# One of eight products of a selective scan moved from VectorE to GpSimd, its operand spread by transfers

## The chip, the core and the metric

The kernel runs on one core of a Trainium2 chip. The metric is device time in microseconds (us) of one execution. Engines are called as in the profile: PE (TensorE), DVE (VectorE), ACT (ScalarE), POOL (GpSimd), SP (SyncE, which here only issues transfers).

## What is computed

A chain of four layers on x of shape (2, 128, 64, 64), fp32: a Mamba-like sequence layer with two blocks, two convolutional attention layers, and a multi-scale fusion. The change lies in the first, of which this is what matters (B = 2 images, L = 4096 tokens, di = 256 inner channels, N = 16 states):

```python
dt, Bm, Cm = jnp.split(u @ xproj_w.T, [R, R + N], axis=-1)
dt = jax.nn.softplus(dt @ dt_w.T + dt_b)
dA = jnp.exp(dt[..., None] * A)
dBu = (dt * u)[..., None] * Bm[:, :, None, :]
def step(h, inp):
    dA_t, dBu_t, C_t = inp
    h = dA_t * h + dBu_t
    y = jnp.einsum('bdn,bn->bd', h, C_t)
    return (h, y)
...
y = ys.transpose(1, 0, 2) + u * ssm_D
y = y * jax.nn.silu(z)
```

Before it stand a layer norm, a projection to u and z and a causal convolution of four taps; after it a projection, a residual, a second layer norm and a feed-forward part with GELU.

## The kernel before

The sequence layer is cut into 32 chunks of 512 tokens: 2 images x 2 blocks x 8 chunks, in this order (`items`). A chunk has 256 x 16 = 4096 pairs of channel and state. They are dealt with in eight *steps* of 512 pairs: a step takes 32 channels (`k = 32 * (s_ % 4)` of half `s_ // 4`), and its tile `h` of 128 partitions x 4 x 512 tokens holds four groups of 32 partitions, each with all 32 channels, times four `m`: 16 states in all. So an operand that depends on channels alone has to be spread, four copies of 32 partitions under one another. For `dt` transfers do that (`spread_dt`, four per step, lines 373 to 378). For dt * u (`dtu`) PE does it, with a matrix of zeros and ones as stationary operand, into the PSUM tile `pdu`, of which there is one (`spread_dtu`, lines 380 to 383). B and C come spread from DRAM in the tiles `bb` and `cb` (`spread_bc`, lines 345 to 354).

A step has four *slots*, one for each `m`; a chunk has 32. Per step: DVE multiplies `bb` by `pdu` into `h` (`times_b`, line 389). Per slot: ACT makes `da`, the exponential of dt times A, four slots ahead into one of four PSUM buffers (`decay`, line 396), and DVE runs the scan along the 512 tokens in place in `h` (`scan`, line 407). At a step's last slot POOL copies the last column as the carry for the next chunk (line 409) and multiplies `h` by `cb` in place (line 410). PE then sums over states, for two steps at a time, into `py` (`y_pair`, line 422, 16 matmul records a pair).

The order on every engine is written out by hand. `slot(i, todo, t_)` issues, for slot t_ of chunk i: at the first slot of a step `spread_dt` for three steps ahead and `spread_dtu` for one ahead, at every second step `y_pair` of the steps three and two back; then the scan, the `decay` of four slots ahead, at the last slot of a step `times_b` of the next step; and last what `background(i)` has put at that slot. So `times_b` of step s stands in slot 4s - 1, and `y_pair` of steps (0, 1), (2, 3), (4, 5), (6, 7) in slots 12, 20, 28 and slot 4 of the next chunk. The background holds the work of neighbouring chunks, among it:

- slots 0 to 5: the convolution of the next chunk (`pu_taps`, line 310), and z of this one (line 323)
- slot 7: `y_out` (line 430) and `gate` on POOL (line 433) of the chunk before; slots 3 to 12: the rest of the feed-forward part of the chunk two back, whose tile `hid` is read last in slot 7 (`ffn_down`, line 467)
- slot 11: `silu`; slots 12 to 15: layer norms (`pc`, line 244), `xproj` (line 339) and its copy `dbl` (line 343), and from it on SP the transfers `dr`, `bb` (slot 14) and `cb` (slot 22)
- slots 15 to 18: `dtproj` (`pt`, line 358), the softplus on ACT (line 364), `dt_end` on POOL (`dtu`, line 370), all for the next chunk
- slots 17 to 21: the variance (`var`, line 258) and reciprocal root of the layer norms, with two small products on POOL (`nt`, line 274, `rs`, line 279) and one step on ACT between (line 275); slots 27 to 29: their spread on PE (`pr`, line 283), the scaling on DVE (line 287) and the shift on ACT (line 300)
- slots 30 and 31: the first half of the feed-forward part (`ffn_up`, line 455) into a new `hid`

The tiles `h` and `hid` share one tag with five buffers, which are handed out in turn: a new one takes the buffer of the fifth allocation before it, and its first writer waits for that one's last reader. A chunk allocates eight `h` and one `hid`.

Ahead of the first chunk stands a prologue (i = -2 and -1) that also loads the 3x3 weights of the next layer (`load_rest`, into three of the five `h` buffers) and folds them on DVE (`fold`, lines 190 to 206, in slots 8 to 10 of i = -1); the folded weights are written to DRAM.

Of the kernel before, what the change touches and what calls it, by code (L numbers as in the profile page):

```python
# [6 lines left out]
F32 = mybir.dt.float32  # L7
AF = mybir.ActivationFunctionType
ALU = mybir.AluOpType
# [4 lines left out]
B, C, H, W = 2, 128, 64, 64  # L14
N = H * W
P = 128
CH = 512
# [50 lines left out]
def tile_conv_seq(ctx: ExitStack, tc, x, consts, vecs, wemb, wlay, wconv, wdt, wqkv, wsmall, wms, out):  # L68
    nc = tc.nc
# [46 lines left out]
    with tc.manual_schedule(), ExitStack() as s:  # L116
# [4 lines left out]
        sp = scans.enter_context(tc.tile_pool(name="l0s", bufs=1, side="right"))  # L121
        bc = scans.enter_context(tc.tile_pool(name="l0bc", bufs=1, space=PSUM, side="right"))
# [15 lines left out]
        def four(g):  # L138
            return fsel[:, g].rearrange("p q d -> p (q d)")
# [30 lines left out]
                nc.vector.tensor_tensor(u[:, k, :], cw[:, KC, :], cw[:, k, :], ALU.mult)  # L170
            wu.append(u), am.append(a)

        raws = []

        def load_rest():
            for which in range(3):
# [13 lines left out]
        def fold(which):  # L190

            g = [raws[which][:, :, k, :] for k in range(3)]
            lo, hi = (sp.tile([P, 3, 3, C], F32, name=n, tag="h", bufs=5) for n in ("ulo", "uhi"))
            tt, ts, stt = nc.vector.tensor_tensor, nc.vector.tensor_scalar, nc.vector.scalar_tensor_tensor
            tt(lo[:, 1], g[0], g[2], ALU.add)
            ts(lo[:, 1], lo[:, 1], -1.0 / 6, None, ALU.mult)
            stt(lo[:, 0], g[1], 1.0 / 6, lo[:, 1], ALU.mult, ALU.add)
            stt(lo[:, 1], g[1], -1.0 / 6, lo[:, 1], ALU.mult, ALU.add)
            stt(hi[:, 0], g[2], 4.0, g[0], ALU.mult, ALU.add)
            ts(hi[:, 0], hi[:, 0], 1.0 / 24, None, ALU.mult)  # L200
            stt(lo[:, 2], g[1], -1.0 / 12, hi[:, 0], ALU.mult, ALU.add)
            stt(hi[:, 0], g[1], 1.0 / 12, hi[:, 0], ALU.mult, ALU.add)
            ts(hi[:, 1], g[0], 0.25, None, ALU.mult)
            nc.vector.tensor_copy(hi[:, 2], g[2])
            for k, u in enumerate((lo, hi)):
                nc.sync.dma_start(ufold[which][:, 9 * k : 9 * k + 9, :], u.rearrange("p s y c -> p (s y) c"))


# [4 lines left out]
        NI, NST, NSL = len(items), 8, 32  # L213
        st = [{} for _ in items]
# [3 lines left out]
        def has(i):  # L218
            return 0 <= i < NI
# [153 lines left out]
        def spread_dt(g):  # L373
            i, s_ = divmod(g, NST)
            o = st[i]["dtb", s_] = sp.tile([P, CH], F32, name="dtb", tag="dtb", bufs=4)
            k = 32 * (s_ % 4)
            for q in range(4):
                nc.sync.dma_start(o[32 * q : 32 * q + 32, :], st[i]["dt"][k : k + 32, s_ // 4, :])

        def spread_dtu(g):  # L380
            i, s_ = divmod(g, NST)
            pdu = st[i]["pdu", s_] = bc.tile([P, CH], F32, name="pdu", tag="bc")
            nc.tensor.matmul(pdu, lhsT=four(s_ % 4), rhs=st[i]["dtu"][:, s_ // 4, :], start=True, stop=True)  # L383

        def times_b(g):
            i, s_ = divmod(g, NST)
            h = st[i]["h", s_] = sp.tile([P, 4, CH], F32, name="h", tag="h", bufs=5)
            pdu = st[i].pop(("pdu", s_))
            nc.vector.tensor_tensor(h, st[i]["bc", 0], pdu.unsqueeze(1).to_broadcast([P, 4, CH]), ALU.mult)  # L389
# [8 lines left out]
        def scan(t):  # L398
            g, m = divmod(t, 4)
            i, s_ = divmod(g, NST)  # L400
            j, gg = divmod(s_, 4)
            b, l, c = items[i]
            if (b, l) not in carries:
                carries[b, l] = sp.tile([P, NJ, 4, 4], F32, name="carry", tag="carry", bufs=2)
                nc.gpsimd.memset(carries[b, l], 0.0)
            h, da = st[i]["h", s_], st[i].pop(("da", s_, m))
            nc.vector.tensor_tensor_scan(h[:, m, :], da, h[:, m, :], carries[b, l][:, j, gg, m : m + 1], ALU.mult, ALU.add)  # L407
            if m == 3:
                nc.gpsimd.tensor_copy(carries[b, l][:, j, gg, :].unsqueeze(2), h[:, :, CH - 1 : CH])  # L409
                nc.gpsimd.tensor_tensor(h, h, st[i]["bc", 1], ALU.mult)  # L410

        def y_pair(g):

            i, s_ = divmod(g, NST)
            j, gg = divmod(s_, 4)
            if gg == 0:
                st[i]["py", j] = yp.tile([P, CH], F32, name="py", tag="y")
            py = st[i]["py", j]
            for m in range(4):
                for k in range(2):  # L420
                    r = 32 * (gg + k)
                    nc.tensor.matmul(  # L422
                        py[r : r + 32, :], lhsT=sel, rhs=st[i]["h", s_ + k][:, m, :], start=(m == 0), stop=(m == 3),
                        tile_position=(0, r),
                    )
# [63 lines left out]
        def background(i):  # L489

            todo = [[] for _ in range(NSL)]

            def at(t, f, *a):
                todo[t].append((f, a))

            n, p, q, r = i + 1, i - 1, i - 2, i + 2
            if has(q):
                at(3, gelu, q)
                at(6, ffn_down, q, (0, 1)), at(7, ffn_down, q, (2, 3)), at(9, ffn_add, q)
                at(11, out_mm, q), at(12, out_add, q)  # L500
            if has(p):
                at(7, y_out, p, 1), at(7, gate, p)
                at(9, mix_out, p), at(11, mix_add, p)
            if has(n):
                at(0, pu_taps, n, 0, (0, 1)), at(1, pu_taps, n, 0, (2, 3)), at(2, pu_out, n, 0)
                at(3, pu_taps, n, 1, (0, 1)), at(4, pu_taps, n, 1, (2, 3)), at(5, pu_out, n, 1)
                at(13, xproj, n), at(14, xproj_out, n), at(14, spread_bc, n, 0), at(22, spread_bc, n, 1)
                at(15, dtproj, n, 0), at(16, dtproj, n, 1), at(17, soft_plus, n), at(18, dt_end, n)
            if has(i):
                at(1, pz_mm, i, 0), at(3, pz_out, i, 0)  # L510
                at(5, pz_mm, i, 1), at(6, pz_out, i, 1)
            if has(i) or has(n):
                at(11, silu, i, n)
            if i == -1:
                at(1, load_rest), at(7, prepare, 1)
                for k in range(3):
                    at(8 + k, fold, k)
                at(19, spread_dtu, 0), at(26, times_b, 0)
            pair = [(k, second) for k, second in ((p, True), (r, False)) if has(k)]
            if has(r):  # L520
                at(10, embed, r), at(11, embed_out, r)
            w, m = {}, len(pair)
            for k, (it, second) in enumerate(pair):
                at(12 + 2 * k, ln_centre, w, k, it)
                at(13 + 2 * k, ln_square, w, k, it)
                at(27, ln_spread, w, k, m), at(28, ln_scale, w, k, it)
                at(29, ln_shift, w, k, it, second)
            if pair:
                at(17, ln_var, w, m), at(18, ln_eps, w, m), at(19, ln_rs, w, m), at(20, ln_newton, w, m), at(21, ln_step, w, m)
            if has(p):  # L530
                for f in range(4):
                    at(30 + f // 2, ffn_up, p, f)
            if has(i):
                at(24, y_out, i, 0)
            return todo
# [5 lines left out]
        NG, NT = NI * NST, NI * NSL  # L541
        def slot(i, todo, t_):
            t = i * NSL + t_
            g, m = divmod(t, 4)
            if m == 0 and 0 <= g + 3 < NG:
                spread_dt(g + 3)
            if m == 0 and 1 <= g + 1 < NG:
                spread_dtu(g + 1)
            if m == 0 and g % 2 == 1 and 0 <= g - 3 < NG:
                y_pair(g - 3)  # L550
            if 0 <= t < NT:
                scan(t)
            if 0 <= t + 4 < NT:
                decay(t + 4)
            if m == 3 and 1 <= g + 1 < NG:
                times_b(g + 1)
            for f, a in todo[t_]:
                f(*a)
        for i in range(-2, NI):
            todo = background(i)  # L560
            for t_ in range(NSL):
                slot(i, todo, t_)
        todo = background(NI)
        for t_ in range(8):
            slot(NI, todo, t_)
# [331 lines left out]
        sp = s.enter_context(tc.tile_pool(name="ats", bufs=1, reuse_waits="tile"))  # L897
        psa = s.enter_context(tc.tile_pool(name="atpa", bufs=2, reuse_waits="tile", space=PSUM))
        psm = s.enter_context(tc.tile_pool(name="atpm", bufs=1, reuse_waits="tile", space=PSUM))
        for now in range(NALL + LAG + 10):  # L900
            r, u = divmod(now, NU)
# [71 lines left out]
    with ExitStack() as s, tc.manual_schedule():  # L973
        sp = s.enter_context(tc.tile_pool(name="mss", bufs=1, reuse_waits="tile"))
# [60 lines left out]
        st = [{} for _ in items]  # L1035
# [433 lines left out]
```

## Time and profile before

| what | us |
|---|---|
| median of 3 runs | 5001.07 (5000.54 to 5005.86) |
| the profiled execution's own time | 5004.69 |
| its span, first to last instruction | 5002.9 |

By stage, busy us in the profiled execution:

| stage, us | PE | DVE | ACT | POOL | granted PE clock |
|---|---|---|---|---|---|
| prologue, 0 to 73 | 36.9 | 31.1 | 23.3 | 9.1 | 0.78 |
| sequence layer, 73 to 2092 | 1807.7 | 1883.2 | 1466.8 | 1427.0 | 0.90 |
| attention layers, 2092 to 4400 | 2257.5 | 1692.6 | 671.8 | 721.6 | 0.99 |
| fusion, 4400 to 5003 | 559.2 | 417.8 | 197.0 | 179.8 | 0.97 |

Busy sums say how much work an engine has, not whether others wait for it. The scans of the 32 chunks start at 73.35 us and end at 2091.56 us. In the profile a group's row gives the source line, engine, operation, the tile written and those read, shape and count, then busy us and mean ns of one, then the idle us of the engine just ahead of it and what released it. In the view in order of time a row begins with start and duration in us; what stands in brackets is the idle time before it and its releaser. PE's rows count records: one product of 128 x 512 fp32 has two.

### The profile page before, as it was taken

What the parts mean: (1) busy time and instruction counts of PE and PEld (TensorE: products, weight loads), DVE (VectorE), ACT (ScalarE), POOL (GpSimd) and SP (SyncE); (2) the same over time, 40 slices, a digit from 0 to 9 for tenths busy, and PEclk for the clock granted to TensorE, in tenths of its full rate; (3) what the DMA queues carried; (4) which work ended last, traced back from release to release, by engine and by line L of the source; (5) the groups of instructions that cost most, each with busy time, mean ns of one, the idle gap of its engine ahead of it and who ended that gap; (6) DMA issues with size and microseconds to landing.
All of it is one profiled execution on the core that took longest, in us unless ns stands there. A gap on an engine that the chain in (4) does not pass through costs nothing. (4 is left out here: it accounts for less than half of the span.)

```text
span 5002.9 us, 48954 instructions
## 1 busy us (share of the span) xinstructions
PE 4661.3 (93%) x14797; PEld 2242.4 (45%) x14797; DVE 4024.6 (80%) x4283; ACT 2358.8 (47%) x3218; POOL 2337.5 (47%) x1974
## 2 busy tenths in 40 slices
PE   5889999999988899899999999999999999999997
PEld 1222222222222222366667766666666666333332
DVE  6999999999999999878886677767776775667776
ACT  4677777777777777522222222233333332323332
POOL 3777776766777777513332133333333332333331
PEclk8898889989999989899999999999999999999998
DMA  6333333322323333214444344434443443000000
GB/s 163 69 68 68 69 71 70 69 65 62 72 67 68 70 73 73 73 53 113 109 110 123 105 112 111 120 95 114 110 100 98 112 113 88 3 7 7 5 7 9
DMA packets 242343, 386.24 MB, mean 77 GB/s; under 512 B 88592, under 2 KB 88992, under 8 KB 233632
## 3 DMA queue, kind: packets, MB, share of 16 engines
q1 hardware_dynamic: 192928, 315.94, 26.0%
q10 hardware_dynamic: 49152, 67.17, 5.4%
q8 instruction: 118, 1.93, 0.2%
q14 instruction: 145, 1.19, 0.1%
HBM read 101.02 MB, written 13.37 MB: 23 GB/s over the span
## 5 line engine op out<-in xcount | busy, mean ns | idle before, releaser
L792 POOL COPY pt<-tr 32x512 f32<-32x512 f32 x1024 | 650.8, 636 | 1437.3 <-DVE tr L785 704.7
L407 DVE TENSOR_TENSOR_SCAN h<-da,carry,h 128x512 f32<-128x512 f32 x1024 | 1241.6, 1266 | 59.7 <-ACT da L396 30.7
L410 POOL TENSOR_TENSOR h<-h,cb 128x2048 f32<-128x2048 f32 x256 | 1160.9, 4535 | 21.0 <-POOL carry L409 0.4
L755 PE MATMUL pq<-k,q 128*128 128x512 f32 x2048 | 962.6, 593 | 7.0 <-DVE sc L760 7.0
L805 PE MATMUL po<-pt,vt 128*128 128x256 f32 x4096 | 965.7, 379 | 2.5 <-DMA pt<-tr 2.5
L770 ACT ACTIVATE sc<-sc,nm 128x2048 f32<-128x2048 f32 x256 | 510.6, 1995 | 912.8 <-DVE nm L766 701.6
L805 PEld LDWEIGHTS po<-pt,vt 128*128 128x128 f32 x4096 | 777.9, 190 | 294.8 <-issue 208.3
L760 DVE TENSOR_SCALAR_CACHE_REDUCE sc<-pq 128x1024 f32<-128x1024 f32 x512 | 625.1, 1222 | 315.6 <-PE pq L755 294.3
L396 ACT ACTIVATE da<-dtb,am 128x512 f32<-128x512 f32 x1024 | 681.5, 684 | 230.5 <-DVE h L407 207.9
L389 DVE TENSOR_TENSOR h<-bb,pdu 128x2048 f32<-128x2048 f32 x256 | 581.7, 2272 | 86.0 <-PE py L422 29.3
L785 DVE STREAM_TRANSPOSE tr<-sc 128x2048 f32<-128x2048 f32 x256 | 591.6, 2311 | 64.6 <-DMA pt<-tr 56.2
L422 PE MATMUL py<-h,sel 128*32 128x512 f32 x2048 | 511.0, 643 | 1.6 <-POOL h L410 1.6
L755 PEld LDWEIGHTS pq<-k,q 128*128 128x128 f32 x2048 | 382.9, 190 | 283.2 <-issue 247.2
L383 PE MATMUL pdu<-dtu,fsel 128*128 128x512 f32 x512 | 325.3, 721 | 117.0 <-DVE h L389 114.8
L422 PEld LDWEIGHTS py<-h,sel 128*32 128x32 f32 x2048 | 115.2, 117 | 415.0 <-issue 409.5
L310 PE MATMUL pu<-xn,wu 128*128 128x512 f32 x512 | 246.2, 614 | 2.6 <-ACT xn L300 1.7
L383 PEld LDWEIGHTS pdu<-dtu,fsel 128*128 128x128 f32 x512 | 95.9, 214 | 322.0 <-DVE h L389 199.5
L409 POOL COPY carry<-h 128x4 f32<-128x4 f32 x256 | 47.8, 187 | 394.5 <-DVE h L407 392.7
L1219 DVE TENSOR_TENSOR ov<-v,pw 128x2048 f32<-128x2048 f32 x64 | 146.2, 2285 | 62.1 <-PE pw L1212 62.1
L1153 PE MATMUL pqkv<-f,ws 128*128 128x512 f32 x384 | 188.2, 615 | 3.0 <-DVE prod L1170 2.3
L1223 POOL TENSOR_TENSOR ov<-ov 128x2048 f32<-128x2048 f32 x16 | 72.6, 4538 | 235.5 <-DVE ov L1219 235.5
L370 POOL TENSOR_TENSOR dtu<-dt,u 128x1024 f32<-128x1024 f32 x32 | 75.1, 2348 | 192.6 <-ACT dt L364 192.6
(259 smaller groups left out, 5266.6 us busy)
## 6 DMA issues: line engine op xcount, KB each, us to landing
pt<-tr SPq DMA_DIRECT2D x2048, 64.0 KB, 2.0
dtb<-dt SPq DMA_DIRECT2D x1024, 64.0 KB, 2.0
pt<-tr ACTq DMA_DIRECT2D x1024, 64.0 KB, 2.2
bb<-dr SPq DMA_DIRECT2D x128, 256.0 KB, 4.4
cb<-dr SPq DMA_DIRECT2D x128, 256.0 KB, 4.6
uw<-ufold SPq DMA_DIRECT2D x12, 576.0 KB, 4.3
uw<-dkept SPq DMA_DIRECT2D x20, 288.0 KB, 3.0
xt<-in_x SPq DMA_DIRECT2D x16, 256.0 KB, 4.6
```

The source lines that it names most:

```text
L383: nc.tensor.matmul(pdu, lhsT=four(s_ % 4), rhs=st[i]["dtu"][:, s_ // 4, :], start=True, stop=True)
L389: nc.vector.tensor_tensor(h, st[i]["bc", 0], pdu.unsqueeze(1).to_broadcast([P, 4, CH]), ALU.mult)
L396: nc.scalar.activation(da, st[i]["dtb", s_], AF.Exp, scale=am[items[i][1]][:, j, gg, m : m + 1])
L407: nc.vector.tensor_tensor_scan(h[:, m, :], da, h[:, m, :], carries[b, l][:, j, gg, m : m + 1], ALU.mult, ALU.add)
L410: nc.gpsimd.tensor_tensor(h, h, st[i]["bc", 1], ALU.mult)
L422: nc.tensor.matmul(py[r : r + 32, :], lhsT=sel, rhs=st[i]["h", s_ + k][:, m, :], start=(m == 0), stop=(m == 3), tile_position=(0, r),)
L755: nc.tensor.matmul(pq[:, i, :], lhsT=sta["q", r, grp][:, it * P : (it + 1) * P], rhs=sta["k"][:, at : at + CH], start=True, stop=True)
L760: nc.vector.tensor_scalar(dst, pq, 1.0, None, ALU.mult, ALU.max, accum_out=sta["mx"][:, c2 : c2 + 1])
L770: nc.scalar.activation(sc, sc, AF.Exp, bias=nm, scale=scale, accum_out=sm[:, hh : hh + 1])
L785: nc.vector.transpose(tr, sta.pop(("sc", r, blk, hh)).rearrange("p (t r f) -> p r t f", r=NB, f=32))
L792: nc.gpsimd.tensor_copy(dst, src)
L805: nc.tensor.matmul(sta["po", r, grp], lhsT=sta["vt"][:, jt, :], rhs=rhs, start=(jt == 0), stop=(jt == N // P - 1))
```

## The change

The step with number 5, the sixth of eight, is taken out of `spread_dtu` and `times_b`. Instead, in slot 5 of each chunk four transfers on SP spread its 32 channels of `dtu` over the 128 partitions of a new tile `dub` (one buffer), and in slot 11 POOL multiplies `bb` by `dub`, broadcast over `m`, into `h`. In the code `at(11, ...)` stands behind the slot's own work, so on POOL it follows the carry and product of step 2. The tile `h` of step 5 is now allocated in slot 11, ahead of that of step 4. In the prologue the writes of the folded weights move out of `fold` (slots 8 to 10) into `fold_out` (slot 23), and the tiles of the second fold take buffers of `bb` and `cb` instead of `h`.

```diff
-            lo, hi = (sp.tile([P, 3, 3, C], F32, name=n, tag="h", bufs=5) for n in ("ulo", "uhi"))
+            tags = (("h", 5), ("h", 5)) if which != 1 else (("bb", 2), ("cb", 2))
+            lo, hi = (sp.tile([P, 3, 3, C], F32, name=n, tag=t, bufs=k) for n, (t, k) in zip(("ulo", "uhi"), tags))
+            folded.append((lo, hi))
...
-            for k, u in enumerate((lo, hi)):
+
+        def fold_out(which):
+            for k, u in enumerate(folded[which]):
                 nc.sync.dma_start(ufold[which][:, 9 * k : 9 * k + 9, :], u.rearrange("p s y c -> p (s y) c"))
...
+        BY_POOL = (5,)
+
+        def spread_pool(i, s_):
+            o = st[i]["dub", s_] = sp.tile([P, CH], F32, name="dub", tag="dub")
+            k = 32 * (s_ % 4)
+            for q in range(4):
+                nc.sync.dma_start(o[32 * q : 32 * q + 32, :], st[i]["dtu"][k : k + 32, s_ // 4, :])
+
+        def times_b_pool(i, s_):
+            h = st[i]["h", s_] = sp.tile([P, 4, CH], F32, name="h", tag="h", bufs=5)
+            dub = st[i].pop(("dub", s_))
+            nc.gpsimd.tensor_tensor(h, st[i]["bc", 0], dub.unsqueeze(1).to_broadcast([P, 4, CH]), ALU.mult)
...
             if has(i):
+                at(5, spread_pool, i, 5), at(11, times_b_pool, i, 5)
...
                 for k in range(3):
-                    at(8 + k, fold, k)
+                    at(8 + k, fold, k), at(23, fold_out, k)
...
-            if m == 0 and 1 <= g + 1 < NG:
+            if m == 0 and 1 <= g + 1 < NG and (g + 1) % NST not in BY_POOL:
                 spread_dtu(g + 1)
...
-            if m == 3 and 1 <= g + 1 < NG:
+            if m == 3 and 1 <= g + 1 < NG and (g + 1) % NST not in BY_POOL:
                 times_b(g + 1)
```

More of the change, by code (lines that the diff above doesn't have):

```diff
@@ L171, in prepare @@
             wu.append(u), am.append(a)
-        raws = []
+        raws, folded = [], []
         def load_rest():
```

## The prediction

> **What bounds the kernel now.** I read the busy sums by stage first. The change touches only the Mamba stage, 73 to 2092 us: 32 chunks of 512 tokens, each of eight steps of four slots, 63.1 us a chunk. There DVE is busy 1883 of 2019 us (93%), POOL 71%, ACT 73%, PE 90%. Next, the costliest groups of the page give the price of each operation (mean ns after the comma):
>
> ```profile
> L407 DVE TENSOR_TENSOR_SCAN h<-da,carry,h 128x512 f32<-128x512 f32 x1024 | 1241.6, 1266 | 59.7 <-ACT da L396 30.7
> L410 POOL TENSOR_TENSOR h<-h,cb 128x2048 f32<-128x2048 f32 x256 | 1160.9, 4535 | 21.0 <-POOL carry L409 0.4
> L389 DVE TENSOR_TENSOR h<-bb,pdu 128x2048 f32<-128x2048 f32 x256 | 581.7, 2272 | 86.0 <-PE py L422 29.3
> L383 PE MATMUL pdu<-dtu,fsel 128*128 128x512 f32 x512 | 325.3, 721 | 117.0 <-DVE h L389 114.8
> ```
>
> Is a 93% busy DVE the bound? Its waits decide that, here of 300 to 1900 us (total us, times, longest):
>
> ```profile
> DVE h L407 <- ACT da L396: 24.1, 37, 1.1
> DVE h L389 <- PE py L422: 22.5, 22, 1.4
> DVE h L389 <- PE pdu L383: 17.2, 35, 0.8
> ```
>
> I counted where in the chunk they lie, over all chunks. The scans of slots 23 or 25 wait for ACT in every chunk but the last (0.8 us a chunk together), and times_b into slots 7, 11 and 31 waits for PE (1.0, 0.5, 0.9 us). So DVE is stopped again and again by others, and what matters is the chain that stops it. One chunk, PE, then DVE, ACT, POOL, in order of time (start, duration):
>
> ```profile
> 1045.13 3.63 PE L422 MATMUL py<-h,sel 128*32 128x512 f32 x16
> 1048.69 1.13 PE L244 MATMUL pc<-xt,kc 128*128 128x512 f32 x2
> ...
> 1073.27 2.07 PE L383 MATMUL pdu<-dtu,fsel 128*128 128x512 f32 x2 [1.49 <-DVE h L389]
> 1075.27 5.28 PE L422 MATMUL py<-h,sel 128*32 128x512 f32 x16
> ```
> ```profile
> 1046.33 2.26 DVE L389 TENSOR_TENSOR h<-bb,pdu 128x2048 f32<-128x2048 f32 x1
> ...
> 1054.92 2.29 DVE L389 TENSOR_TENSOR h<-bb,pdu 128x2048 f32<-128x2048 f32 x1 [0.75 <-PE pdu L383]
> 1057.31 4.95 DVE L407 TENSOR_TENSOR_SCAN h<-da,carry,h 128x512 f32<-128x512 f32 x4
> ```
> ```profile
> 1056.36 1.27 ACT L364 ACTIVATE dt<-pt,vec 128x512 f32<-128x512 f32 x2
> ...
> 1066.08 0.72 ACT L275 ACTIVATE nt<-nt,c 2x512 f32<-2x512 f32 x1 [2.67 <-POOL nt L274]
> ```
> ```profile
> 1046.47 0.19 POOL L409 COPY carry<-h 128x4 f32<-128x4 f32 x1 [2.85 <-DVE h L407]
> 1046.74 4.55 POOL L410 TENSOR_TENSOR h<-h,cb 128x2048 f32<-128x2048 f32 x1
> 1057.70 2.35 POOL L370 TENSOR_TENSOR dtu<-dt,u 128x1024 f32<-128x1024 f32 x1 [6.41 <-ACT dt L364]
> 1060.26 4.55 POOL L410 TENSOR_TENSOR h<-h,cb 128x2048 f32<-128x2048 f32 x1
> 1064.78 1.26 POOL L274 TENSOR_TENSOR nt<-nt,ve 2x512 f32<-2x512 f32 x1
> ```
>
> The reader is to see a **loop**. PE works without a wait from pdu of step 0 (1008.42, a chunk earlier) through py (ends 1048.76) to pc. ACT then works its list without a gap over 0.5 us to softplus (dt, ends 1057.63). POOL, idle 6.41 us for it, makes dtu, the product of step 4 and nt; ACT makes nt at 1066.08 and the da of slot 25, ready at 1067.39; the scan of slot 25 starts at 1067.40. Step 7's times_b (line 389, 1070.95 to 1073.21) frees pdu, and PE starts the next round at 1073.27: 64.85 us after 1008.42. Where slot 25 doesn't wait, slot 23 does: its da comes behind softplus too. **Step 5's times_b (1054.92) does not lie on this loop.**
>
> **What the Trainium skill says.** "GPSIMD Engine Reference", Performance versus the Vector engine: a tensor_tensor of 2048 fp32 takes 4497 ns on GpSimd, 2293 on VectorE; the trace agrees (4535, 2272). "SBUF — State Buffer", Who interferes with whom: a VectorE instruction with two SBUF inputs contends with a GpSimd instruction that reads SBUF. The trace agrees at the start, where fold's two-input addition (line 195) takes 2.47 us under POOL's dtu against 0.55 us before; in this stage times_b and the scan read one SBUF tensor and one of PSUM, and times_b shows 2259 to 2290 ns throughout, so more POOL work slows neither. "TensorE: Matmul & The Clock Gate", Part 1: after an idle window of about 3.4 us PE runs at half clock. The trace agrees in kind: py takes 5.28 us behind waits, 3.63 otherwise. "DMA: Bandwidth & Descriptors", Queues, rings and completion order: each DMA engine takes descriptors in ring order; no row here shows that by itself, and I use it for the start only.
>
> **The change, part by part.**
> Removed from DVE: 32 x 2.272 = 72.7 us, and its pdu wait (0.2 us a chunk on average). Off the loop: what DVE saves is waited for at slots 23 and 25. Worth 0, but in the last chunk, which prepares no successor and shows no wait past slot 7: there 2.3 us.
> Removed from PE: the pdu of step 5, two matmuls of about 0.5 us spacing, at 1053.69, behind pc and just before the second pt. Softplus needs that pt at 1056.36 and has it at 1055.87, so 0.
> Added to POOL: 32 x 4.54 us, behind the product of step 2 (ends 1043.62). New order in this chunk: step 5's product 1043.65 to 1048.19; step 3's carry and product to 1052.9 instead of 1051.29; dtu still at 1057.70. The 4.54 us are covered by POOL's 2.85 + 6.41 us of idle, and 4.7 us stay over. The broadcast operand is not in the trace; half the price to twice the price still leaves dtu on time (4.7 - 4.5 = 0.2 us at twice). Without that cover each us would enter the loop.
> Added to SP: 128 transfers of 64 KB, about 0.6 us of issue each (2.4 us a chunk), placed before the xr and dtb issues, on which SP waits for buffers anyway; 2.0 us to land, in slot 5 for slot 11. Worth 0.
> **Added wait on DVE.** h has five buffers, taken in order of allocation. Step 5 now allocates before step 4, so step 4's times_b (slot 15) needs the buffer of step 0, which py of steps 0 and 1 (slot 12) frees; before, it took one free since slot 7. In this chunk it slides from 1046.33 to 1048.86 (2.5 us); over all chunks py ends from 0.2 us before to 2.4 us after slot 15's scan. Queued behind it on DVE are the scans, and ACT's da of slots 20 and 21, which need scans 16 and 17: scan 16 would end at 1048.86 + 2.39 + 1.26 = 1052.5 against da 20 at 1053.74, scan 17 at 1053.7 against 1054.35. A margin of 0.58 us remains in the tightest full chunks, 1.2 in the loosest. With step 5's times_b gone, DVE reaches slot 23 at 1059.6, when its da is ready at 1060.96: the scan starts as before. Worth 0; bounds 0 and 1.0 us a chunk (rival two).
> Fold's writes move from slots 8 to 10 to slot 23 of the prologue. SP now waits for line 204 (until 60.2) before it issues dr at 60.65, though dbl is there at 47.9; dr and bb would come some 12 us earlier and step 0 could start near 63 instead of 73.35. But dtb of step 1 now queues behind 3.5 MB of fold at about 236 GB/s (measured there) and lands near 77, as now (77.48). The scan of step 1 moves from 80.44 to about 78.5: -2 us, bounds -8 (no queueing) and +3.
> Sum: 0 x 31 chunks - 2.3 - 2 = -4.3 us. The profiled execution took 5004.69 us (span 5002.9 and 1.8 around), 3.6 over the median 5001.07; from it 5000.4, from the median **4997**.
>
> **The rivals.**
> One, DVE is the bound after all: the sum of 93% speaks for it, the waits on ACT in every chunk against it. 5001 - 72.7 - 4 = 4924.
> Two, slower: the new wait of step 4's times_b on py. If da 20 and 21, and with them softplus and dtu, move with it, the whole slide counts. Summed over the chunks with the wake-up time it is 8 x 0.7 + 9 x 1.6 + 4 x 2.5 + 3.5 = 33 us, so 5001 - 4 + 33 = 5030. It decides from a slide of ACT's input of more than 0.58 us beyond what I replayed; for it speaks how thin this is, against it that pc and py come from the same PE queue and so move together.
> Three, POOL gets late (its product at twice the price or dub late): dtu is then late by what exceeds 4.7 us; 1 us a chunk gives 5028. PE's longer idle at slot 17 (2.3 instead of 1.2 us) could also leave it at half clock longer; a py at 5.28 instead of 3.63 in the loop costs 1.65 us, in half the chunks 26 us.
> That the change does not do what it says: the instruction order shows 32 products on POOL and as many fewer on DVE, so no.
>
> **How the numbers follow.** Forecast (4990 to 5005) 0.56; rival one or a part of it 0.17; rival two 0.17, rival three 0.10. A difference under 0.2% (10 us) is about what a measurement of this kernel can't tell from none. Faster by more: 0.17 and 0.04 of the forecast's edge, 0.21; slower: 0.25, some of both late rivals staying under 10 us; same: 0.54. Range 4975 to 5031: the forecast, both slower cases and the near end of rival one.
>
> **What would show it.** Right: times_b of step 4 waits for py, up to 2.5 us; waits on da at slots 23 and 25 grow to 2 to 3 us a chunk; DVE's busy time falls by 73 us and the stage's length by under 5; POOL still waits 3 to 5 us for dt. Wrong: softplus starts later behind pc than now (rival two), POOL no longer waits for dt (rival three), or the waits at 23 and 25 don't grow and chunks get 2 us shorter (rival one).

## The result and the profile after

| kernel | median of its runs, us | ratio to before, 95% interval |
|---|---|---|
| before | 5005.83 | 1 |
| changed | 4997.72 (4993.12 to 5001.39) | 0.9987 [0.9979, 0.9995] |
| changed, in a later comparison (before 5003.16) | 4998.79 (4993.27 to 5001.62) | 0.9990 [0.9984, 0.9997] |

By the ratios the change makes the kernel some 5 to 7 us faster, 0.1%. The profiled execution has a span of 4994.5 us. First the costliest groups of the changed kernel's page (busy us, mean ns, then the idle time ahead of the group and what ended most of it), and below them its waits from 300 to 1900 us (total us, times, longest):

```profile
L425 DVE TENSOR_TENSOR_SCAN h<-da,carry,h 128x512 f32<-128x512 f32 x1024 | 1240.1, 1265 | 104.8 <-ACT da L414 80.1
L407 DVE TENSOR_TENSOR h<-bb,pdu 128x2048 f32<-128x2048 f32 x224 | 509.5, 2275 | 102.9 <-PE py L440 62.0
```
```profile
POOL dtu L374 <- ACT dt L368: 87.0, 25, 4.7
...
DVE h L425 <- ACT da L414: 64.4, 56, 1.9
...
DVE h L407 <- PE py L440: 46.9, 39, 2.5
```

Line 407 runs 224 times where it was 256, at the same 2.27 us, so DVE has lost 72.2 us of work. Both rows have gained idle time: 45.1 us ahead of the scans, 16.9 ahead of times_b. Work has turned into waiting. The waits on `da` have grown from 24.1 to 64.4 us, those on `py` from 22.5 to 46.9. The same chunk as in the prediction, DVE and then POOL in order of time:

```profile
1040.40 2.29 DVE L407 TENSOR_TENSOR h<-bb,pdu 128x2048 f32<-128x2048 f32 x1 [2.45 <-PE py L440]
1042.79 7.16 DVE L425 TENSOR_TENSOR_SCAN h<-da,carry,h 128x512 f32<-128x512 f32 x6
1051.20 1.28 DVE L425 TENSOR_TENSOR_SCAN h<-da,carry,h 128x512 f32<-128x512 f32 x1 [1.25 <-ACT da L414]
1053.54 1.28 DVE L425 TENSOR_TENSOR_SCAN h<-da,carry,h 128x512 f32<-128x512 f32 x1 [1.05 <-ACT da L414]
```
```profile
1035.12 4.69 POOL L401 TENSOR_TENSOR h<-bb,dub 128x2048 f32<-128x2048 f32 x1
...
1049.24 2.35 POOL L374 TENSOR_TENSOR dtu<-dt,u 128x1024 f32<-128x1024 f32 x1 [4.69 <-ACT dt L368]
```

Step 4's times_b (slot 15) waits 2.45 us for `py`. Six scans follow without a break where step 5's times_b used to stand between them, and DVE reaches slots 22 and 23 too early: 1.25 and 1.05 us of waiting. POOL has made the product and still waits 4.69 us for `dt`. I added up DVE's waits of over 0.15 us by slot, from the same trace, as a mean over the third to the 31st chunk (us; where nothing is said a slot's wait is that of a scan on `da`):

| slot | before | changed |
|---|---|---|
| 0 | 0.18 | 0.17 |
| 7, 11 (times_b, on PE) | 0.92, 0.43 | 0.92, 0.43 |
| 15 (times_b of step 4, on PE) | 0 | 0.99 |
| 18 | 0.06 | 0 |
| 19 (times_b of step 5, on PE) | 0.24 | is gone |
| 22, 23 | 0, 0.34 | 1.51, 0.91 |
| 25 | 0.52 | 0.12 |
| 31 (times_b, on PE) | 0.88 | 0.89 |
| sum | 3.57 | 5.94 |

The sum has grown by 2.4 us, what the product took with its gap. The lengths of the chunks agree: from the third to the 30th each is as long as before to 0.1 us, whether 61.4 or 66.2. All that was gained lies at the ends. The first scan starts at 61.52 instead of 73.35 us; the first chunk gives 4.0 us of that back, the second gains 0.9, so the third starts 8.7 us earlier. The last is 2.6 us shorter (56.5 for 59.1). The scans end at 2080.71 instead of 2091.56 us. The stages behind, which the change doesn't touch, take 2913.8 us here and 2911.3 in the trace of before; over the profiled kernels of this study they take 2909 to 2917, so a single span is good to some 4 us.

What closes the loop in that chunk of the changed kernel is shown by the chain of work that ended last, followed back through it (start, us, what; "issue" is time without a visible cause):

```profile
1047.90 0.70 ACT dt L368
1048.60 0.04 issue
1048.64 3.59 PE var L262 x4
1052.23 0.02 issue
1052.25 0.68 ACT ve L266
1052.93 0.58 ACT da L414
...
1053.54 1.28 DVE h L425
...
1062.57 2.19 DVE h L407
1064.76 0.04 issue
1064.80 2.08 PE pdu L387 x2
```

Read it upwards: PE's pair for the next chunk's step 0 waits for step 7's times_b, that for the scan of slot 23, that for a `da`, and that stands in ACT's queue behind the eviction of `var`. PE's matmuls for `var` wait for softplus, and softplus hangs on the matmuls of PE's list, which starts with the pair for step 0. Step 5's product (slot 19) isn't in it. The view goes the same way in 11 of the 29 chunks from the third to the 31st; in most others it follows POOL over stretches without a visible cause, and shows nothing.

For the prologue, here is ACT's `da` for step 1, and below it two stretches of 5 us (busy us and number of instructions of PE, PEld, DVE, ACT and POOL, then the granted clock, the busy share of the DMA engines and GB/s):

```profile
70.09 1.91 ACT L414 ACTIVATE da<-dtb,am 128x512 f32<-128x512 f32 x3 [6.54 <-DMA dtb<-dt]
```
```profile
60.00:65.00 5.00, 4.00 (x5) 1.79 (x6) 5.00 (x5) 1.91 (x3) 0.00 (x0) 0.50 1.02 420
65.00:70.00 5.00, 4.22 (x8) 1.43 (x6) 3.50 (x3) 0.00 (x0) 3.45 (x2) 0.83 0.96 355
```

`dtb` of step 1 does stand behind the fold's writes, and step 1's scan waits for it until 70.82 (80.44 before). But in these two stretches the transfers run at 355 to 420 GB/s.

### The profile page after: what moved, and what is told of

It reads as the page before. It is cut to its first block, busy times and chain, and to the rows that moved or that the text cites. A ratio compares the mean times of both kernels' runs of the same rounds, so it can differ in the third digit from the quotient of the medians.

```text
span 4994.5 us, 48945 instructions
## 1 busy us (share of the span) xinstructions
PE 4642.8 (93%) x14733; PEld 2236.1 (45%) x14733; DVE 3952.1 (79%) x4251; ACT 2358.5 (47%) x3218; POOL 2480.6 (50%) x2006
## 4 chain that ended last, share of the span: by engine, by line
PE 56%; POOL 16%; DVE 11%; issue 8%; ACT 4%; DMA 2%; SPq 2%; ACTq 0%; DVEq 0%; POOLq 0%
PE po L824 14%; PE pq L774 14%; POOL h L428 11%; PE py L440 3%; DVE tr L804 3%; PE pa L671 2%; PE pf L1145 2%; DMA pt<-tr 2%; PE pu L314 2%; DVE h L425 2%; POOL h L401 2%; PE pqkv L1172 2%; SPq L815 2%; PE pdu L387 1%; PE pw L1231 1%
## 5 line engine op out<-in xcount | busy, mean ns | idle before, releaser
L407 DVE TENSOR_TENSOR h<-bb,pdu 128x2048 f32<-128x2048 f32 x224 | 509.5, 2275 | 102.9 <-PE py L440 62.0
L387 PE MATMUL pdu<-dtu,fsel 128*128 128x512 f32 x448 | 291.2, 737 | 104.8 <-DVE h L407 102.4
L1242 POOL TENSOR_TENSOR ov<-ov 128x2048 f32<-128x2048 f32 x16 | 72.5, 4534 | 235.5 <-DVE ov L1238 235.5
L262 PE MATMUL var<-sq,kc 128*2 128x512 f32 (+1 forms) x128 | 109.2, 1000 | 64.6 <-ACT dt L368 63.2
```

## The experiments

The kernel before, measured beside them each time, took 5004.53 us with the first four, 5003.16 with the next two (and the changed kernel again), 5004.54 with the three after that and 5004.61 with the last two.

**The prologue alone.** The fold's edits stay, no product moves.

```diff
-        BY_POOL = (5,)
+        BY_POOL = ()
...
-                at(5, spread_pool, i, 5), at(11, times_b_pool, i, 5)
```

> The kernel before with only the prologue part of the change: the folded weights are written to DRAM in slot 23, the second fold's tiles lie in bb's and cb's buffers; step 5's product stays on DVE. Theory (the chunks turn on a loop through softplus, step 5's product is off it): the whole head start is here, the scans begin about 12 us earlier and the third chunk about 8.7 us earlier, as in the changed kernel; the end gains nothing; time 6 to 9 us below before. Rival (the chunks themselves give the gain, a little each, saving and new wait nearly balanced): about 0.

Measured: 4997.24, ratio 0.9985 [0.9978, 0.9991], 7.3 us. That is the gain of the whole change. In its trace the third chunk starts 12.5 us earlier than before, not 8.7 as expected: the first chunk keeps its length (59.3 us), so the 4.0 us that the changed kernel gives back there come with the moved product.

**The moved product alone.** The fold's writes go back to slots 8 to 10, its tiles to the buffers of `h`.

```diff
-            tags = (("h", 5), ("h", 5)) if which != 1 else (("bb", 2), ("cb", 2))
...
+            lo, hi = (sp.tile([P, 3, 3, C], F32, name=n, tag="h", bufs=5) for n in ("ulo", "uhi"))
...
-                    at(8 + k, fold, k), at(23, fold_out, k)
+                    at(8 + k, fold, k), at(8 + k, fold_out, k)
```

> The changed kernel with the folded weights written in slots 8 to 10, with h's buffers for all three folds, as before: step 5's product alone is moved to POOL. Theory: chunks 2 to 30 as long as before to 0.1 us each, the last one about 2.5 us shorter; time about 2.4 us below before. Rival (a little gain in each chunk): 8 us below.

Measured: 5004.91, ratio 1.0001 [0.9993, 1.0009]. Moving 72 us of DVE's work to POOL gains nothing that can be measured; the interval of about 4 us either way leaves room for the 2.6 us of the last chunk, which its trace shows too (56.5 us). The scans of that trace end 4.8 us earlier than before (2086.77), but the stages behind took 2917.0 us in it, so it doesn't show whether this gain reaches the kernel's time.

**Without the new wait on py.** POOL's instruction moves to slot 16, so step 5's buffer is allocated after step 4's.

```diff
-                at(5, spread_pool, i, 5), at(11, times_b_pool, i, 5)
+                at(5, spread_pool, i, 5), at(16, times_b_pool, i, 5)
```

> The changed kernel, but POOL's product of step 5 stands in slot 16 instead of 11, so that its tile is allocated after that of step 4 and step 4's product no longer waits for py. Theory: the wait for py in slot 15 (1.0 us a chunk) is gone and comes back as wait for POOL or for da in slots 20 to 23; the chunks keep their length, time as the changed kernel, 8 us below before. Rival two (this wait eats what DVE saves): 33 us faster than the changed kernel, 41 below before.

Measured: 5001.54, ratio 0.9992 [0.9984, 1.0000]. The wait in slot 15 is gone (0 instead of 0.99 us), and the time doesn't fall; scan 20 waits instead, 2.3 us a chunk, for POOL's product:

```profile
1044.63 2.46 DVE L425 TENSOR_TENSOR_SCAN h<-da,carry,h 128x512 f32<-128x512 f32 x2 [1.73 <-POOL h L401]
```

One wait has been exchanged for a longer one, so this run alone doesn't decide on rival two. What decides is softplus, which by that rival would move with the wait: it stays in its place, as the table below shows.

**The product twice.** POOL makes it two times over.

```diff
-            nc.gpsimd.tensor_tensor(h, st[i]["bc", 0], dub.unsqueeze(1).to_broadcast([P, 4, CH]), ALU.mult)
+            for _ in range(2):
+                nc.gpsimd.tensor_tensor(h, st[i]["bc", 0], dub.unsqueeze(1).to_broadcast([P, 4, CH]), ALU.mult)
```

> The changed kernel with POOL's product of step 5 made twice (same result written again), 4.54 us more on POOL a chunk. The changed kernel leaves POOL idle for dt 3.5 us a chunk on average, so dtu, the product of step 4 and nt come about 1 us later. Theory (loop through POOL): between 0 and 1 us a chunk slower than the changed kernel, so 8 us below to 23 us above before, likeliest 5 above. If POOL is not on the loop at all (rival one or two): as the changed kernel, 8 below.

Measured: 5043.61, ratio 1.0075 [1.0062, 1.0089], 39 us over before and, by the ratios, some 44 over the changed kernel: 1.4 us a chunk. POOL and ACT in a later chunk:

```profile
1319.91 9.39 POOL L402 TENSOR_TENSOR h<-bb,dub 128x2048 f32<-128x2048 f32 x2
...
1333.97 2.35 POOL L374 TENSOR_TENSOR dtu<-dt,u 128x1024 f32<-128x1024 f32 x1
```
```profile
1331.32 1.26 ACT L368 ACTIVATE dt<-pt,vec 128x512 f32<-128x512 f32 x2
```

`dt` is there at 1332.58, and POOL comes to `dtu` straight from its own work at 1333.97 (nothing stands in brackets), 1.4 us late. In the kernel before and in the changed one `dtu` starts 0.1 us after softplus every time; here 1.0 to 2.0 us after it in 26 of 32. It is on time in the 15th to the 18th chunk, in the second and in the prologue. The prediction had been worked out in the 16th; the expectation had used the average idle time, 3.5 us, and 4.54 us for the product, which takes 4.62 to 4.69 here. In the changed kernel POOL's idle time ahead of `dtu` is 4.7 us in those four chunks, 4.5 in the second, but 2.7 to 3.8 us in the others. POOL's lateness goes into the time at once: POOL lies on the loop.

**Two links of the loop loosened, in the kernel before and in the changed one.** `dtu` is made behind POOL's Newton step of the layer norm (`nt`, `rs`), and ACT's `ve` a slot later, behind the `da` of slot 23.

```diff
-                at(15, dtproj, n, 0), at(16, dtproj, n, 1), at(17, soft_plus, n), at(18, dt_end, n)
+                at(15, dtproj, n, 0), at(16, dtproj, n, 1), at(17, soft_plus, n)
...
-                at(17, ln_var, w, m), at(18, ln_eps, w, m), at(19, ln_rs, w, m), at(20, ln_newton, w, m), at(21, ln_step, w, m)
+                at(17, ln_var, w, m), at(19, ln_eps, w, m), at(19, ln_rs, w, m), at(20, ln_newton, w, m), at(21, ln_step, w, m)
+            if has(n):
+                at(18 if i == -1 else 21, dt_end, n)
```

> The kernel before with two links of the loop loosened, nothing else: dtu stands on POOL in slot 21 behind nt and rs instead of in slot 18 ahead of step 4's product (first chunk excepted), and ACT's ve in slot 19 behind the da of slot 23 instead of ahead of it. Theory: DVE's waits for da in slots 23 and 25 (0.8 us a chunk) shrink, the chunks get up to 0.8 us shorter: 15 to 25 us below before. Rival (loop elsewhere, DVE or PE): 0.

> The changed kernel with the same two links loosened. Theory: the time that DVE saved and lost again in waits for da in slots 22, 23 and 25 (2.5 us a chunk) comes free in good part, since DVE reaches them earlier than in the kernel before: 1.3 to 2.3 us a chunk below the changed kernel, that is 50 to 80 us below before, and clearly more than the same loosening gives to the kernel before. Rival two (the saving is eaten by the wait for py): the same gain as in the kernel before, about 25 us, and 30 below before. Rival (loop elsewhere): 8 below before.

The changed kernel, unedited, ran beside them:

> The changed kernel itself beside these three: 8 us below before.

Measured: 4998.79 for it; before so loosened 4970.02, ratio 0.9934 [0.9921, 0.9948], 33 us; changed so loosened 4971.44, ratio 0.9936 [0.9924, 0.9949], 32 us. In the first, no scan of slots 23 and 25 waits for `da` any more: at least one of the two links was on the loop. How the 33 us divide between POOL's and ACT's wasn't tried. The second missed my expectation, that now DVE's saved time would show; it came out where I had put rival two (the same gain as in the kernel before). The places of some operations in the chunk tell what happened (us after the chunk's first scan, mean over the third to the 31st chunk, from the traces):

| | before | changed | before, loosened | changed, loosened |
|---|---|---|---|---|
| scan 16 starts | 30.39 | 31.47 | 30.39 | 31.47 |
| scan 20 starts | 37.88 | 36.19 | 37.85 | 36.19 |
| softplus ends | 38.09 | 38.09 | 38.08 | 38.09 |
| `da` of slot 22 is ready | 40.09 | 40.10 | 40.08 | 40.09 |
| scan 22 starts | 40.28 | 40.13 | 40.26 | 40.12 |
| `da` of slot 25 is ready | 47.82 | 47.82 | 46.24 | 46.48 |
| scan 25 starts | 47.85 | 47.87 | 47.01 | 47.10 |
| length of the chunk | 63.31 | 63.33 | 62.29 | 62.52 |

With the change scan 16 is 1.1 us late by step 4's wait for `py`, and softplus ends where it did: rival two is refuted, with and without the loosening. DVE reaches slot 20 1.7 us earlier than before, but slot 22 only 0.14 us earlier, because its `da` stands on ACT straight behind softplus. There the saving is lost, and the loosening doesn't touch that link.

The rest is lost at PE. In the changed kernel loosened, step 6's times_b waits for its pair on PE, which stands behind the matmuls for `var`, which wait for softplus:

```profile
1034.38 0.70 ACT dt L368
1035.08 0.04 issue
1035.12 3.57 PE var L262 x4
1038.69 1.59 PE pdu L387 x2
1040.28 0.02 issue
1040.31 2.30 DVE h L407
```

As far as the view follows it, the chain goes through `var` in 20 of the 29 chunks and by the `da` of slot 22 in 8. In the kernel before, loosened, it goes through `var` in 11; step 7's times_b stands in it in 25, step 5's in 2. So even there step 5's product is hardly ever on the loop. The same matmuls in one chunk of each kernel, before loosened and changed loosened:

```profile
1040.96 2.45 PE L258 MATMUL var<-sq,kc 128*2 128x512 f32 x4 [1.23 <-ACT dt L364]
```
```profile
1035.12 3.57 PE L262 MATMUL var<-sq,kc 128*2 128x512 f32 x4 [2.04 <-ACT dt L368]
```

Over all chunks with four such records, PE stands still for 2.0 to 2.1 us ahead of them in the traces with step 5's pair gone and takes 3.42 to 3.50 us for them; with the pair in place it is 1.4 and 2.80 to 2.93 us. This costs little here: the chunks of the changed kernel loosened are 0.2 us longer than those of the kernel before loosened. The Trainium skill, "TensorE: Matmul & The Clock Gate", Part 1, gives some 3.4 us as the window after which an idle PE is slowed, and says that the window runs free. In the trace of the changed kernel the granted clock falls to 0.5 twice a chunk (58 times in these 29), and in the 12 us before each fall PE never stood still for more than 2.7 us, so a single gap as long as the page's window isn't needed. That the longer gap is what slows `var` isn't shown: in the chunk of the changed kernel that was followed above, the clock fell at 1046.3 us, before PE stood still at 1046.7.

Six buffers for `h` instead of five would take away the waits for `py`. They do not fit (124.3 kB a partition are needed where 118.5 are left), so what these waits cost in the loosened kernels was not measured.

**Step 7's product in place of step 5's.** As much is taken from DVE and given to POOL as by the change, only from a place behind the waits of slots 22 to 25.

```diff
-        BY_POOL = (5,)
+        BY_POOL = (7,)
...
-                at(5, spread_pool, i, 5), at(11, times_b_pool, i, 5)
+                at(5, spread_pool, i, 7), at(16, times_b_pool, i, 7)
```

> As the changed kernel, but it is step 7's product with B that GpSimd makes (its instruction in slot 16, its transfers in slot 5), and step 5's is back on VectorE. As much is taken from VectorE and added to GpSimd as by the change. My theory: what counts is whether the product lies behind the da of slots 22 to 25, that is on the loop from TensorE over softplus to VectorE and back; step 5's (slot 19) lies ahead of it, step 7's (slot 27) behind it. Then a chunk gets up to 2.3 us shorter; TensorE's next pair (py of steps 4 and 5) then waits for GpSimd's product of step 5 in its place, so 1.2 to 2.3 us a chunk, beside the prologue's 8: 4920 to 4955. Rival: GpSimd's own time is the bound, or TensorE's 90% is, whichever product is taken away from VectorE: 4990 to 5003, as the changed kernel.

Measured: 4955.23, ratio 0.9902 [0.9889, 0.9916], 49 us. 7 of these are the prologue's, so the product is worth some 42, 1.3 us a chunk. That is just past the slow end of my range (4955), and 35 us from the rival's. DVE shows where the other microsecond of the 2.3 went:

```profile
1036.78 2.29 DVE L407 TENSOR_TENSOR h<-bb,pdu 128x2048 f32<-128x2048 f32 x1 [2.48 <-PE py L440]
```

Step 7 now allocates ahead of step 5, so step 6's times_b (slot 23) gets the buffer of step 2 and waits for the `py` of steps 2 and 3, 2.24 us on average. It is the same kind of wait as the change put into slot 15. That it counts here is argued, not tried: from this wait to slot 31 no scan waits over 0.15 us, so it is passed on to the end of the chunk.

**The same, loosened.**

> As the run with step 7's product on GpSimd, and dtu made after GpSimd's Newton step of the layer norm, with ScalarE's var eviction behind the decay of slot 23 (the loosening that gave 33 us to the kernel before and 32 to the changed one). My theory: with GpSimd off the loop and step 7's product off it too, both gains add up, 73 and 32 us beside the prologue's 8, until TensorE's own list (some 57 us a chunk busy) binds: 4890 to 4925. Rival: after the loosening VectorE's times_b and TensorE bind each other in slots 31, 7 and 11 whatever is moved (that would be why the loosening gave the changed kernel no more than the kernel before): 4960 to 4972, no gain over the loosening alone.

Measured: 4952.80, ratio 0.9899 [0.9886, 0.9913]. The gains don't add: the wait of slot 23 takes 2.74 us a chunk, and no scan of slots 22 to 25 waits for `da` any more. My theory fell here; the rival named nearly the right outcome (little over the loosening, 4960 at the least) in the wrong place, since times_b in slot 31 doesn't wait at all.

**Prologue and loosening, no product on POOL.** The edits are those of the first experiment and of the loosening together.

> The kernel before with the change's prologue (fold's writes in slot 23) and the loosening, no product on GpSimd. My theory: the two gains add, 8 + 33: 4960 to 4964, that is below the changed kernel with the loosening (4971), so that the moved product costs a few us once GpSimd isn't on the loop. Rival: they don't add, 4970, as both with and without the product.

Measured: 4964.25, ratio 0.9920 [0.9906, 0.9933]. The two gains, 7 and 33 us, add. Whether step 5's product on POOL costs anything in the loosened kernel isn't settled: 0.9936 [0.9924, 0.9949] overlaps with this, though in the traces the chunks are 0.2 us longer with it.

**Step 6's product, with and without the loosening.** Step 6 in slot 16 needs no buffer early, so no new wait on `py` comes with it.

```diff
-        BY_POOL = (5,)
+        BY_POOL = (6,)
...
-                at(5, spread_pool, i, 5), at(11, times_b_pool, i, 5)
+                at(5, spread_pool, i, 6), at(16, times_b_pool, i, 6)
```

> As the run with step 7's product on GpSimd, with step 6's in its place (times_b of slot 23). In the order of buffers step 7 then comes after it and takes the one of steps 2 and 3, which is free by slot 27, so no times_b waits for py in slots 15 or 23 as it did for step 4 and step 6 in the two other choices. My theory: slot 23 lies behind the da of slots 22 and 23 but ahead of that of slot 25, which waits for GpSimd's Newton step; where slot 25 sets the loop nothing is gained, elsewhere up to 2.3 us. With the prologue's 8: 4955 to 4985, a gain between those of step 5 (0) and step 7 (41). Rival: any product but step 5's gains alike, and what step 7's lost in the wait on py is gained besides: 4925 to 4950.

> The same with the loosening, so that slot 25 doesn't wait for GpSimd's Newton step. My theory: step 6's times_b now lies on what is left of the loop (softplus, the scans of slots 22 to 27, TensorE), without the wait on py that held the run with step 7's product; from the 4964 of prologue and loosening 1 to 2.3 us a chunk: 4890 to 4932. Rival: VectorE and TensorE bind each other near 61.5 us a chunk whichever product is moved (the run with step 7's product gained only 2 us from the loosening): 4948 to 4964.

Measured: step 6 alone 4995.37, ratio 0.9983 [0.9975, 0.9990], which is the prologue and nothing else; loosened 4945.68, ratio 0.9878 [0.9863, 0.9893], 59 us, the fastest kernel of all. Neither lies in my range. DVE with step 6's product alone:

```profile
1055.08 1.28 DVE L425 TENSOR_TENSOR_SCAN h<-da,carry,h 128x512 f32<-128x512 f32 x1 [1.24 <-ACT da L414]
...
1058.98 3.63 DVE L425 TENSOR_TENSOR_SCAN h<-da,carry,h 128x512 f32<-128x512 f32 x3 [1.98 <-ACT da L414]
```

What was saved is waited for at slots 24 and 25, 1.21 and 1.52 us a chunk where before had 0 and 0.52; the `da` of slot 25 is ready 47.79 us after the chunk's first scan, as before (47.82). So slot 25, behind POOL's nt, closes the loop in every chunk or follows too close for a gain, also where before shows a wait only at slot 23; I had allowed for half of the chunks. Loosened, slot 25 waits no more, and step 6's product is worth 0.0042, the difference from prologue and loosening alone (0.9920), or 21 us, 0.7 us a chunk. The remaining 1.6 us are found at slot 24, where the scan waits 1.56 us on average:

```profile
1030.17 1.28 DVE L425 TENSOR_TENSOR_SCAN h<-da,carry,h 128x512 f32<-128x512 f32 x1 [1.43 <-ACT da L414]
```

In the chunk before this one two things end within 0.1 us of each other ahead of that `da`, ACT's list behind softplus and the transfer of `dtb` behind that of `bb`; which of them binds wasn't tried.

## Why the prediction was right, and where not

The forecast was 4997 and the change brought 4997.72. The agreement to 1 us is in part chance: the kernel before took 5005.83 us beside it, 4.8 over the median that I had started from. As a difference, I gave -4.3 us; measured are -6.5 (0.9987 of 5005), within -2.5 and -10.5. Two terms missed in opposite directions: the prologue brought 7.3 us where I had said 2, and the product nothing that can be measured where I had said 2.3.

- **The loop, and "step 5's times_b does not lie on this loop": right, and shown.** Chunks of equal length, nothing gained from the product alone (1.0001), 42 us from step 7's, which does lie there. The same removed work is worth 0 (steps 5 and 6) or 42 us (step 7) by its place. As I drew it, the loop was that of one chunk: with the change, in this chunk, it closes by `var`, `ve` and the `da` of slot 23, one of the two ways that I had named.
- **DVE's saved time is waited for: right in sum, slightly wrong in place.** 2.4 us more a chunk: 0.99 at slot 15, forecast there, the rest at slots 22 (1.51) and 23 (0.91 for 0.34) rather than at 23 and 25. The link that the prediction left out is the `da` of slot 22 straight behind softplus. DVE's busy sum fell from 4024.6 to 3952.1 us, 72.5 where I had said 73.
- **POOL's 4.54 us are covered: right. "Even at twice the price dtu is on time": wrong.** One product took 4.65 to 4.69 us. In the chunk that I replayed 4.69 us of idle were left, as forecast (4.7). But that chunk has the most to spare: 2.7 to 3.8 us nearly everywhere else, and the doubled product cost 44 us. The step that failed is to take the reserve from one chunk; POOL's idle time ahead of `dtu` was 4.5 to 5.5 us in most chunks of before where I had read 6.41, and the smallest sets how much can be added. So rival three was nearer than its 0.10 said.
- **The wait of step 4's times_b on py: right in size and price.** 2.45 us against 2.5; without it nothing is gained, and with it softplus ends 38.09 us after the chunk's first scan, as before. Rival two is refuted.
- **PE's pair removed, 0: right, by cover alone.** Softplus does end in its place. But PE stands still longer before `var` and takes 0.6 us longer for it (the second half of rival three), so the `da` of slot 23 is ready at 42.29 us after the chunk's first scan where before it was 41.81, and the scan of slot 23 starts 0.45 us later, not "as before". The `da` of slot 25, at 47.82 in both, covers that.
- **The last chunk, -2.3: 2.6 us shorter in the trace.** So it is in three traces (the changed kernel twice, the moved product alone). That it shortens the kernel isn't shown: the product alone measured 1.0001.
- **The prologue, -2: mis-sized.** The prologue alone brings 7.3 us. Order and mechanism were as foretold: `dr` is issued at 46.2 instead of 60.65 us, the first scan starts at 61.5 (I had said 63), and step 1 waits for `dtb` behind fold's writes. The term that failed is the 236 GB/s at which they would drain. That was the rate in a stretch where DVE was still folding and handing out one write at a time, and the DMA engines were busy for 0.59 of it. With all six writes issued one after the other the window shows 355 to 420 GB/s at a share of 0.96 to 1.02, `dtb` is there at 70.1 instead of 77, and step 1's scan starts at 70.8 instead of 78.5. The near bound of -8 ("no queueing") is close to what came.
- **No contention of DVE and POOL in the stage: right.** times_b takes 2275 ns on average, as before (2272).

## What to carry to other kernels

Work taken off the busiest engine is worth what it is worth at its place: ask which wait follows it, and if one does in every round, move the operation behind that wait instead; here that made 42 us out of 0. To find it, set the places of one round's operations side by side, counted from its first: where the two kernels meet again, the saving has been waited away. When a wait is removed, look for the engine that is late next, and don't add two gains before both have run together. Take a reserve from the tightest of all rounds, not from the one in view, and a rate of transfer only from a stretch in which nothing else paces it.

## What was not expected

- With one pair of matmuls taken off PE, its next four records, those of `var`, took 3.47 us on average where before took 2.88. Why isn't shown.
- Softplus ends 38.1 us after the chunk's first scan in all four kernels of the table, whatever DVE gained or lost ahead of it.
- POOL's product with a broadcast operand took 4.65 to 4.69 us in slot 11, 4.54 to 4.61 in slot 16 (step 7's) and 4.61 to 4.67 there in the loosened kernel (step 6's), beside 4.53 on average for the plain product of the same size. What makes the difference of 0.1 us wasn't tried.
- Six writes of the folded weights, 3.5 MB, with the `dtb` transfers behind them, kept the DMA engines full at up to 420 GB/s.
